# A decoder's cross attention: mask tables, normalized rows and bias additions made row by row during self attention and kept in DRAM

## The chip, the core and the metric

The kernel runs on one core of a Trainium2 chip. Its time is that of one launch on the device, in microseconds (us). The engines named below are the Tensor engine (PE, with PEld for its weight loads), the Vector engine (DVE), the Scalar engine (ACT), GpSimd (POOL) and the sync engine (SP), which issues nearly all DMA transfers. [...]

## What is computed

The reference is a decoder of two layers on x of 8 batch rows (B = 8) of 512 positions and 256 channels, all in float32. Only its first two steps matter here:

```python
x = x + _L0_attn_ref(_layernorm(x), Wq, Wk, Wv, gamma)             # self attention
x = x + _L0_xattn_ref(_layernorm(x), ctx, ctx, adj, mask, ...)     # cross attention, 16 heads of 16
```

Cross attention projects the normalized rows to queries and the context to keys and values. Its scores get the adjacency matrix added, are masked by batch row, go through a softmax over the 512 keys, weigh the values, and are projected out with a bias. After it come a local-attention transformer of two layers, an integer-quantized attention, a second cross attention and a mixture of eight experts.

## The kernel before, in words

Since exp(s + a) = exp(s) * exp(a), the kernel multiplies the exponentials of the scores by a table `share` = (mask is not 0) * exp(adj). The table depends on the batch row and is 128 partitions x 4 key tiles x 512 queries, 1 MB. The exponential of adj is taken once (`adj`, in place).

*First stage* (`stage_self_attention`, L1310). It loops over the batch rows; in iteration b it makes the scores of row b (L1395), transposes (L1362), projects (L1384) and makes the values (L1372) of row b + 1, and weighs row b (L1407). PSUM results go to SBUF alternately by ACT and DVE (`evac`, L97 to L103: sa_xnT, sa_u, sa_h). For each of four tiles, DVE takes the reciprocal of the sums and forms sa_o (L1412 to L1415), and POOL adds it to x (L1417). `means` (L1419) then takes on DVE the layer-norm statistics of the finished row for cross attention: BN statistics (L143), and a Newton iteration of tiny instructions (L1477 to L1481).

*Cross attention* (`stage_cross_attention`, L1528) is a generator. `Ahead.step(3)` in each iteration of the first stage runs it three `yield`s further, so its loads, its constants and the preparation of row 0 are spread over the first stage. After that it owns the engines. It runs 16 steps a batch row (`scores`, `soften`, `weigh`; 128 steps). A step makes four heads' scores for one key tile (PE, L1724), takes two exponentials of 128x1024 (ACT, L1735), multiplies both by `share` (DVE, L1736), and weighs the values of two steps before (PE, L1752). During the 16 steps of row b, `prepare(b + 1)` supplies small groups of calls, one group a step: loads (step 0), keys K (steps 2 and 4), the four normalizations (steps 5 and 6, L157), the bias addition `behind` (step 7, POOL, L1623), transposes T of the rows (7 and 8), queries Q (9 and 10), values V, and the four mask products M (`share`, steps 7, 9, 11, 13, DVE, L1612). These calls are `paced`: they are issued behind the multiplies of a step before.

Four steps of `weigh` give one tile of outputs and sums. The sums go through DRAM (`inverted`: sums L3302, x_sums L3303, reciprocal x_inv on DVE three steps later L3306, invs L3307) and are spread to x_wide by DMA (L1776). POOL multiplies by it (L1769). `project_out` (L1782) projects the row in steps 11 to 14 of the next row; DVE adds it to x (L1790) and takes the statistics of the next stage (L1495 to L1508). The finished x is also written to DRAM (`away`, L1797).

The buffers that matter: `x_xn` (normalized rows), `x_mask` and `x_xnT` have one or two, the tables one per parity of the batch row (`x_share0`, `x_share1`), the PSUM tag `pj` has one bank in cross attention and two in the first stage, `po` one and two. Tile pools insert the waits: a tile that takes a buffer waits for all uses of the tile before it. The order of the instructions on each engine is made by the scheduler when the program is built.

## Time and profile before

| | us |
|---|---|
| median of three runs | 3036.18 (3035.45 to 3040.28) |
| the profiled execution | 3039.56 |
| its span in the profile | 3037.8 |
| mean granted clock of PE | 0.972 of full speed |
| PE busy | 2832.6 (93%) |
| DVE busy | 2039.3 (67%) |
| ACT busy | 1191.5 (39%) |
| POOL busy | 388.1 (13%) |
| first stage ends (last weighing matmuls, L1407) | 204.2 |
| a row of cross attention (first key projection to that of the next row) | 50.7, 54.3, 54.5, 53.6, 57.9, 53.5 |

The profile is that of one execution. Its page lists busy times by engine, the span in 40 slices, the DMA queues, the chain of work that ended last, and groups of instructions by line; closer queries give the same for any window. In a timeline row, the columns are start, duration (both us), engine, line, operation, output and inputs with their shapes, and the count; the bracket gives the idle time of the engine just before and what ended it. In a row for a window, each engine has its busy time and, in brackets, its instructions, then come PE's granted clock, the mean busy share of the 16 DMA engines, and GB/s.

### The profile page before, as it was taken

The page shows a single profiled execution, that of the slowest core. Times are in us where ns is not written, and L with a number is a line of the kernel's source. Part 1 is how long each engine was busy: PE and PEld are TensorE (multiplying, and loading weights), DVE is VectorE, ACT ScalarE, POOL GpSimd, SP SyncE. Part 2 cuts the span into 40 slices and gives each one's busy share as a digit, 9 for nine tenths or more (in the row PEclk, how much of TensorE's full clock was granted, in tenths as well). Part 3 has the DMA queues.
Part 4 walks back from the last instruction along what each step waited for, and adds up shares of the span by engine and source line. Part 5 has one row for each costly group of instructions (what it writes and reads, how often), then busy time and mean ns, then how long its engine had stood idle before and what let it go on. Part 6 is the DMA issues. An engine that isn't in the chain of part 4 may idle for free. (4 is left out here: it accounts for less than half of the span.)

```text
span 3037.8 us, 39774 instructions
## 1 busy us (share of the span) xinstructions
PE 2832.6 (93%) x14929; PEld 1511.4 (50%) x14944; DVE 2039.3 (67%) x4546; ACT 1191.5 (39%) x1687; POOL 388.1 (13%) x357
## 2 busy tenths in 40 slices
PE   8999999979999999999999989998796999997998
PEld 5653333225555556555555556564444344444665
DVE  7458998977776784356776788548797766664110
ACT  2237776744444431124444431113364444441111
POOL 1111111100011110000101111101211012121111
PEclk9999999988999999999999999999897999997999
DMA  7011212101000011001000011001332132313331
GB/s 246 1 35 50 72 51 62 42 18 57 15 23 23 15 32 36 0 1 37 22 22 17 21 46 63 21 7 63 106 132 91 43 105 78 112 58 97 102 140 61
DMA packets 130694, 168.71 MB, mean 56 GB/s; under 512 B 51761, under 2 KB 79666, under 8 KB 128443
## 3 DMA queue, kind: packets, MB, share of 16 engines
q1 hardware_dynamic: 126394, 154.48, 16.3%
q0 software_dynamic: 4096, 11.59, 1.0%
q8 instruction: 119, 1.95, 0.3%
q14 instruction: 85, 0.69, 0.1%
HBM read 113.12 MB, written 47.50 MB: 53 GB/s over the span
## 5 line engine op out<-in xcount | busy, mean ns | idle before, releaser
L1889 PE MATMUL pj<-w,la_hT 128*128 128x512 f32 x720 | 334.2, 605 | 5.2 <-ACT la_qkT L1942 4.5
L1736 DVE TENSOR_TENSOR x_e<-x_e,x_share 128x1024 f32<-128x1024 f32 x256 | 315.9, 1277 | 14.3 <-ACT x_e L1735 14.1
L1735 ACT ACTIVATE x_e<-sc 128x1024 f32<-128x1024 f32 x256 | 249.2, 1023 | 83.8 <-PE sc L1724 83.8
L1889 PEld LDWEIGHTS pj<-w,la_hT 128*128 128x128 f32 x720 | 132.6, 191 | 153.4 <-issue 115.6
L2016 DVE TENSOR_TENSOR la_e<-sc,la_mask 128x1024 f32<-128x1024 f32 (+1 forms) x128 | 135.3, 1084 | 103.6 <-PE sc L2007 103.6
L3320 POOL TENSOR_TENSOR la_oT<-la_o,x_wide 128x512 f32<-128x512 f32 x64 | 97.7, 1538 | 753.1 <-DMA x_wide<-invs 678.6
L2945 ACT ACTIVATE ma_e<-sc,ma_bias 128x1024 f32<-128x1024 f32 x128 | 135.6, 1110 | 145.9 <-PE sc L2939 131.4
L2233 ACT ACTIVATE lf_gate<-pj,lf_b 128x512 f32<-128x512 f32 (+1 forms) x82 | 56.3, 687 | 333.3 <-PE pj L2212 318.0
L2020 ACT ACTIVATE la_e<-la_e 128x1024 f32<-128x1024 f32 (+1 forms) x128 | 117.5, 946 | 152.6 <-DVE la_e L2016 151.6
L2212 PE MATMUL pj<-lf_hnT,w 128*128 128x512 f32 (+1 forms) x368 | 171.4, 593 | 2.0 <-DVE lf_hid L2238 2.0
L1752 PE MATMUL po<-x_e,x_v 128*32 128x512 f32 x1024 | 140.7, 622 | 33.7 <-DVE x_e L1736 29.7
L2212 PE MATMUL sc<-lf_hnT,w 128*128 128x512 f32 x336 | 157.7, 592 | 0.0
L1724 PE MATMUL sc<-x_q,x_k 32*128 32x512 f32 x1024 | 152.9, 647 | 1.7 <-DVE sa_ok L1448 1.4
L2284 PE MATMUL po<-w,lf_hid 128*128 128x256 f32 x640 | 149.0, 379 | 0.0
L2238 DVE SCALAR_TENSOR_TENSOR lf_hid<-sc,lf_b,lf_gate 128x512 f32<-128x512 f32 x70 | 52.4, 749 | 136.4 <-PE sc L2212 133.4
L2027 PE MATMUL po<-la_e,la_v 128*64 128x256 f32 (+1 forms) x1024 | 125.8, 370 | 7.0 <-ACT la_o L2044 6.3
L2007 PE MATMUL sc<-la_qkT 64*128 64x256 f32 (+1 forms) x1024 | 128.9, 375 | 1.2 <-DVE la_e L2016 0.6
L2284 PEld LDWEIGHTS po<-w,lf_hid 128*128 128x128 f32 x640 | 117.8, 190 | 21.2 <-issue 7.4
L2939 PE MATMUL sc<-ma_qT,ma_kT 64*128 64x512 f32 x512 | 127.3, 615 | 0.4 <-ACT ma_e L2945 0.4
L2962 PE MATMUL po<-ma_e,ma_v 128*64 128x512 f32 x512 | 125.7, 612 | 0.0
L2070 PE MATMUL pj<-w,la_oT 128*128 128x256 f32 x512 | 121.0, 383 | 2.0 <-DVE lf_t L1480 0.7
L1905 DVE TENSOR_REDUCE la_ss<-la_sq 128x16 f32<-128x1024 f32 x64 | 77.7, 1215 | 65.8 <-ACT la_sq L1896 65.8
(500 smaller groups left out, 5173.6 us busy)
## 6 DMA issues: line engine op xcount, KB each, us to landing
x_wide<-invs SPq DMA_DIRECT2D x184, 128.0 KB
w<-in_f_w_dram SPq DMA_DIRECT2D x16, 1024.0 KB
kv<-kv_o SPq DMA_DIRECT2D x56, 256.0 KB
slots<-x_empty SPq DMA_DIRECT2D x8, 1028.0 KB
x_mask<-in_x_maskT_dram SPq DMA_DIRECT2D x8, 1024.0 KB
ma_kT<-kv SPq DMA_DIRECT2D x8, 1024.0 KB
ma_v<-kv SPq DMA_DIRECT2D x8, 1024.0 KB
ex_rows<-slots SPq DMA_DIRECT2D x7, 1028.0 KB
```

The source lines that it names most:

```text
L1724: nc.tensor.matmul(pair[r // 2][:, r % 2, :], d["k"][rows, g, kt * P : (kt + 1) * P], d["q"][rows, e, g, :], start=True, stop=True,)
L1735: nc.scalar.activation(ex, d["e"][rest][p], AF.Exp)
L1736: nc.vector.tensor_tensor(ex, ex, d["share"][:, kt, :].unsqueeze(1).broadcast_to([P, 2, 512]), ALU.mult)
L1752: nc.tensor.matmul(d["po"][32 * r : 32 * r + 32, :], d["v"][:, kt, 8 * g + 2 * r + e, :], ex[r // 2][:, r % 2, :], start=(kt == 0), stop=( ...
L1889: nc.tensor.matmul(ps, d["hT"][:, k, i * P : (i + 1) * P], wqkv[:, k, j * S : (j + 1) * S], start=(k == 0), stop=(k == 1),)
L2007: nc.tensor.matmul(both[half][:, r, jj * 256 : jj * 256 + to - j * P], d["qkT"][rows, 4 + c, j * P : (j + 1) * P], d["qkT"][rows, c, j * P ...
L2016: nc.vector.tensor_tensor(ex[:, :, :n_cols], ps[:, :, :n_cols], mask[:, :n_cols].unsqueeze(1).broadcast_to([P, 2, n_cols]), ALU.add,)
L2027: nc.tensor.matmul(out[:, j * P : to], lhsT(j), ex[:, jj * 256 : jj * 256 + to - j * P], start=(j == 0), stop=(j == 3), skip_group_check=True,
L2212: nc.tensor.matmul(ps[:m, :], w1[:, k, at : at + m], held[b]["hnT"][:, k, :], start=(k == 0), stop=(k == 1))
L2284: nc.tensor.matmul(ps[:, :C], held[b]["hid"][:, f, i * P : (i + 1) * P], w2[:, f, :], start=(f == 0), stop=False,)
L2939: nc.tensor.matmul(both[m // 2][:, r, :], d["k"][rows, c, kt * P : (kt + 1) * P], d["q"][rows, c, :], start=True, stop=True,)
L2945: nc.scalar.activation(ex, ps, AF.Exp, bias=bias[:, b * NST + kt : b * NST + kt + 1], scale=0.125)
```

## The change

The mask products, the normalizations and the bias additions leave `prepare`. A new function `keep(b)` makes them for one batch row as soon as `means(b)` has its statistics: it loads the mask into the tile that will hold the table, normalizes the four tiles, writes them to DRAM (`xn_kept`), adds the bias on POOL, forms the four products in place, and writes the table to DRAM (`x_tables`). `rows_done` calls it from the first stage, once the constants (`adj`, `bias`) exist. The tile is `x_tab` for odd rows; for even rows it has the tag `x_share0`, which the table of even rows in cross attention has too. The normalized rows pass through `x_xn`, one buffer, which `prepare` uses too. `prepare` now loads the table (step 2 of the row before) and the rows (step 0) instead of making them.

```diff
                 if b > 0:
                     means(b - 1)
+                    self.rows_done(b - 1)
                     ahead.step(3)
             means(B - 1)
+            self.rows_done(B - 1)
...
+    def rows_done(self, b):
+        self.due.append(b)
+        while self.due and self.keep:
+            self.keep(self.due.pop(0))
...
+        xn_kept = self.alloc(self.dram, [B, P, NST * C], F32, "xn_kept")
+        tables = self.alloc(self.dram, [B, P, NST * S], F32, "x_tables")
...
+        def keep(b):
+            share = self.alloc(first, [P, NST, S], F32, "x_tab" if b % 2 else "x_share0", bufs=1)
+            mask = share.bitcast(I32)
+            nc.sync.dma_start(mask, t["x_maskT"][b].rearrange("(k p) q -> p k q", p=P))
+            x = self.x[:, b * NST : (b + 1) * NST, :]
+            xn = self.alloc(first, [P, NST, C], F32, "x_xn", bufs=1)
+            for i in range(NST):
+                self.normalize(xn[:, i, :], x[:, i, :], self.x_ln, b * NST + i)
+            nc.sync.dma_start(xn_kept[b], flat(xn))
+            nc.gpsimd.tensor_tensor(x, x, bias.unsqueeze(1).broadcast_to([P, NST, C]), ALU.add)
+            for k in range(NST):
+                nc.vector.scalar_tensor_tensor(
+                    share[:, k, :], mask[:, k, :], 0.0, adj[:, k, :], ALU.not_equal, ALU.mult
+                )
+            nc.sync.dma_start(tables[b], flat(share))
+
+        self.keep = keep
+        while self.due:
+            keep(self.due.pop(0))
...
-                d["mask"] = self.alloc(first, [P, NST, S], I32, "x_mask", bufs=1)
-                nc.sync.dma_start(d["mask"], t["x_maskT"][b].rearrange("(k p) q -> p k q", p=P))
...
+            def share():
+                d["share"] = self.alloc(own, [P, NST, S], F32, f"x_share{b % 2}", bufs=1)
+                nc.sync.dma_start(flat(d["share"]), tables[b])
...
                 d["xn"] = self.alloc(first, [P, NST, C], F32, "x_xn", bufs=1)
+                nc.sync.dma_start(flat(d["xn"]), xn_kept[b])
...
             yield [load, rows]
             yield []
-            yield [K[0]]
+            yield [K[0], share]
             yield []
             yield [K[1]]
-            yield [normals[0], normals[1], V[0]]
-            yield [normals[2], normals[3], V[1]]
-            yield [behind, T[0], M[0]]
+            yield [V[0]]
+            yield [V[1]]
+            yield [T[0]]
             yield [T[1], V[2]]
-            yield [Q[0], M[1]]
+            yield [Q[0]]
             yield [Q[1]]
-            yield [V[3], M[2]]
-            yield []
-            yield [M[3]]
+            yield [V[3]]
```

More of the change, by code (lines that the diff above doesn't have):

```diff
@@ L1526, in clear_slots @@
         self.sent = []
+    def rows_done(self, b):
+        self.due.append(b)
+        while self.due and self.keep:
+            self.keep(self.due.pop(0))
     def stage_cross_attention(self, ahead):
         nc, t = self.nc, self.t
+        self.due, self.keep = [], None
+        xn_kept = self.alloc(self.dram, [B, P, NST * C], F32, "xn_kept")
+        tables = self.alloc(self.dram, [B, P, NST * S], F32, "x_tables")
         wq, wk, wv, wo = self.load_cross_attention()
@@ L1586, in stage_cross_attention, with flat @@
         held = {}
+        def flat(x):
+            return x.rearrange("p a n -> p (a n)")
+        def keep(b):
[16 more added lines that the diff above has]
+            keep(self.due.pop(0))
         empty = self.alloc(pool, [P, self.WIDE], F32, "x_empty", bufs=1)
@@ L1607, in load @@
                 )
-            def share(k):
-                if k == 0:
-                    d["share"] = self.alloc(own, [P, NST, S], F32, f"x_share{b % 2}", bufs=1)
-                nc.vector.scalar_tensor_tensor(
-                    d["share"][:, k, :], d["mask"][:, k, :], 0.0, adj[:, k, :], ALU.not_equal, ALU.mult
-                )
-            x = self.x[:, b * NST : (b + 1) * NST, :]
-            normals = [
-                lambda i=i: self.normalize(d["xn"][:, i, :], x[:, i, :], self.x_ln, b * NST + i)
-                for i in range(NST)
-            ]
-            def behind():
-                nc.gpsimd.tensor_tensor(x, x, bias.unsqueeze(1).broadcast_to([P, NST, C]), ALU.add)
+            def share():
+                d["share"] = self.alloc(own, [P, NST, S], F32, f"x_share{b % 2}", bufs=1)
+                nc.sync.dma_start(flat(d["share"]), tables[b])
             def rows():
                 d["xn"] = self.alloc(first, [P, NST, C], F32, "x_xn", bufs=1)
+                nc.sync.dma_start(flat(d["xn"]), xn_kept[b])
                 d["xnT"] = self.alloc(first, [P, 2, S], F32, "x_xnT", bufs=1)
@@ L1671, in prepare @@
             V = [lambda i=i: values(i) for i in range(NST)]
-            M = [lambda i=i: share(i) for i in range(NST)]
             T = [lambda c=c: turn(c) for c in range(2)]
```

## The prediction

> **What bounds the kernel now.** I read the page's chain of waits first: the Tensor engine (PE) holds 20% of it and the rest is a few per cent, so the end of each stage is set by PE and by whatever PE waits for. Only two stages are touched, so I cut the start of the span into the first stage and the rows of cross attention (a row of cross attention is 16 steps, recognised by the first key projection of L1642 at 266.4, 320.7, 375.2 us and so on).

> ```profile
> core 0: us, PE busy (x) PEld busy (x) DVE busy (x) ACT busy (x) POOL busy (x), PEclk, DMA share, GB/s
> 24.00:204.00 180.00, 179.26 (x649) 114.61 (x647) 93.58 (x380) 42.58 (x73) 24.15 (x31) 1.00 0.26 81
> ...
> 266.40:320.70 54.30, 51.23 (x315) 17.08 (x312) 48.85 (x65) 39.06 (x48) 8.00 (x3) 1.00 0.21 63
> 320.70:375.20 54.50, 51.35 (x317) 17.13 (x313) 51.10 (x73) 39.52 (x49) 7.87 (x3) 1.00 0.22 61
> 375.20:428.80 53.60, 51.26 (x317) 17.10 (x313) 50.21 (x73) 39.42 (x49) 8.38 (x3) 1.00 0.22 61
> ```

> The first stage has PE busy for 179.3 of 180 us: any stall of PE there is paid in full, though the Vector engine (DVE) is only half busy. A cross-attention row has both full: PE 51.3, DVE about 51 of 54.5. So relief of DVE is worth at most what PE idles, 54.5 - 51.3 = 3.2 us a row. PE's waits over six rows (266.4 to 594 us) say the same, all on DVE:

> ```profile
> engine line waited for: us in total, times, longest us
> PE po L1752 <- DVE x_e L1736: 9.2, 10, 2.8
> PE pj L1785 <- DVE x L1790: 4.0, 7, 0.7
> PE po L1752 <- DVE lt_ln_t L1506: 3.4, 5, 0.7
> ```

> That is 16.6 us, and row 0 (from 215.7) adds 0.3, 0.6 and 1.9.

> **What leaves cross attention.** While row b is computed, row b+1 is prepared, for b = 0 to 6 (row 0's own was prepared in the first stage already). Each time four mask products (L1612), four normalizations (L157) and one bias addition on GpSimd (POOL) go:

> ```profile
> L1612 DVE SCALAR_TENSOR_TENSOR x_share<-x_mask,x_adj 128x512 f32<-128x512 int32 x4 | 2.7, 680 | 0.0
> L157 DVE TENSOR_SCALAR x_xn<-x,x_ln_mean,x_ln_rstd 128x256 f32<-128x256 f32 x4 | 2.4, 644 | 0.0
> ```

> That is 5.1 us of DVE a row. The bias addition's price lies elsewhere:

> ```profile
> 69.96 2.40 POOL L1623 TENSOR_TENSOR x<-x,x_bias 128x1024 f32<-128x1024 f32 x1 [1.27 <-DVE x_bias L1584]
> ...
> 335.69 5.04 POOL L1623 TENSOR_TENSOR x<-x,x_bias 128x1024 f32<-128x1024 f32 x1 [3.47 <-DVE x_xn L157]
> ```

> It takes 2.4 us in the first stage and 5.0 in a busy row, and the multiplies beside it stretch: four in 6.30 us at 338.9, where pairs alone take 2.29. [...] by the row it loses 6.30 - 4.58 = 1.7. I take the row: about 6.8 us of DVE a row goes.

> But PE gets back only idle time whose cause goes. In the row from 320.7: 0.37 us at 343.0 (behind a mask product and the stretched multiplies) goes, 0.54 at 363.5 (L1790 queued behind the fourth mask product) goes; 0.45 at 359.8 stands behind a multiply stretched by another POOL operation, 1.11 at 371.4 behind L3306, which waits 0.96 us for the DMA of x_sums, 0.69 behind the Newton steps of the next stage: these stay. So 0.9, say 1.0 us a row: rows 2 to 6 give 5 us. In row 0 the 1.9 us stand behind an x_sums DMA that was late because the 1 MB mask load ran ahead of it; with that load gone I give it 1.4, and the 0.6 also goes: 2. Relief **-7 us**. Bounds: 3 (only half of this) and 16 (all idle of rows 0 and 2 to 6, 2.7 + 3.2 + 2.3 + 3.8 + 2.1 + 2.0).

> **Where the work lands.** The built program gives the order on each queue, and it differs from the words of the change. x_share0 holds row 0's reloaded table until row 0 is done, and it is also the scratch tile for rows 2, 4 and 6. So their twelve mask products are not made in the first stage but inside row 1, each four after a load of the mask into that one tile, and each load after the write of the table before. Likewise x_xn has one buffer, held by row 0 until its transposes at 139.9 us; so the normalizations of rows 1 to 4 come together at about 144 to 159 us.

> *First stage, DVE blocked on its own writes.* In row 5's scores DVE's queue now reads: normalize row 1 (4), later row 2 (4), row 3 (4), the sa_xnT eviction, row 4 (1), the sa_u eviction, row 4 (3). Each group waits for the 512 KB write of the one before. In the trace of before:

> ```profile
> 147.15 0.17 DVE L1424 COPY x_ln_rstd<-x_ln_rstd 128x4 f32<-128x4 f32 x1
> 151.32 0.69 DVE L103 COPY sa_xnT<-pj 128x512 f32<-128x512 f32 x1 [4.00 <-PE pj L1362]
> ...
> 152.12 0.19 PEld L1384 LDWEIGHTS pj<-sa_xnT,sa_wu 128*128 128x128 f32 x1 [0.24 <-DVE sa_xnT L103]
> ```

> DVE had 4.0 us free and PE took the eviction at once (no slack). A 512 KB write: the "away" write was issued at 313.25 and its bytes were through by 315.5; a small write takes 1.7 us from issue (sums, 269.07) to the next queue entry that needs it (270.77), so 1.7 + 1.4 = 3.1 us. Row 1's group (4 x 0.36 = 1.5 us) ends DVE's work at 148.7, row 2's at 150.2, row 3's can start at 150.2 + 3.3 = 153.5 and ends at 155.0: sa_xnT 3.6 us late. **+3.6** (bounds 1 and 7, by one write more or less). sa_u's wait then falls inside PE's own shift.

> *First stage, the mask products of rows 1, 3, 5, 7* (2.7 us each). Put on DVE's timeline of before: row 1's, at 38.7, push an eviction of po, 0.3 us; row 3's wait for a mask that SP issues only after the table of row 1 is written (42.0 + 4.6 + 5.5 = about 53), about 1.0 us before sa_u; row 5's fall into 70.4 to 75, where 1.07 us are free before sa_xnT: 1.0 with the gaps of the Newton chain; row 7's stand between two releases of po (two banks) at 86 to 90: 1.6. **+3.9** (bounds 1 and 8). The bias additions, 2.4 us each, fit into POOL's gaps of 6 to 18 us between the x additions. SP's new waits hold up only slot clearing and next weights there; neither is due.

> *Boundary.* Row 7's four normalizations stand between the last statistics (211.2 us) and the first multiply (211.31), for which PE was waiting (3.69 us idle at 213.8): 4 x 0.36 = **+1.5**.

> *Row 1.* One chain decides, since the tile is one: load the mask, four products (2.7 us), write the table, load the next mask, and so on. A 1 MB mask load that was issued at 254.50 shows its length:

> ```profile
> 254.00:255.00 1.00, 0.90 (x8) 0.16 (x8) 1.00 (x2) 1.00 (x3) 0.00 (x0) 1.00 0.00 0
> ...
> 257.00:258.00 1.00, 1.00 (x12) 0.21 (x8) 1.00 (x2) 1.00 (x2) 0.00 (x0) 1.00 1.00 367
> ...
> 260.00:261.00 1.00, 1.00 (x12) 0.31 (x8) 1.00 (x2) 0.94 (x2) 0.00 (x0) 1.00 0.01 2
> ```

> The bytes are through by 259.6, so I count 5.5 us to use; a write is 1.7 + 2.9 = 4.6 (1 MB at 367 GB/s). From row 0's last multiply (261.3): mask 267.0, products 269.7, written 274.4, mask 279.9, products 282.6, written 287.2, mask 292.7, products 295.4, and then the multiply of step 22, ready at 297.7. DVE stands still meanwhile, and behind it wait the multiplies that PE's weighing needs: step 17's by 271.6 (ready 272.0), step 20's by 281.9 (ready 284.9), step 22's by 288.3 (it waited until 289.3). So PE ends 9.4 us late there, **+8.4** beyond its old idle; later steps only lose slack that PE-bound rows have. [...] my five transfers are 25.7 us[...] With 1.2 us more a transfer it is +14. [...]

> *Reloads.* Each row now loads its table (1 MB) and its rows (512 KB) from DRAM. A table is issued at step 2 of the row before and first used 14 steps (some 46 us) later, the rows after the last transposes and used most of a row later: 5.5 and 3.1 us, hidden, zero. They stand in SP's queue among the x_wide and x_sums transfers, whose reciprocal comes three steps (10 us) later; the mask load that goes had the same size there. If that cover fails, 1 us a row, 6 in all; the same at the gain side, if the mask loads were what made x_sums late. After cross attention PE's and ScalarE's order is unchanged.

> **Sum.** -7 + 3.6 + 3.9 + 1.5 + 8.4 = +10.4 us on the profiled execution's 3039.6 (span 3037.8 and 1.8 around it): 3050.0. That execution lies 3.4 above the median 3036.2, so the median becomes 3046.6.

> **Rivals.** 0.2% (6 us) is about what a measurement of this kernel can tell from no change.

> *Forecast, chance 0.5:* about 3046.6; by its bounds 3040 to 3053.

> *Slower still, 0.15.* The transfers are longer than one alone shows, because they meet slot clearing (DMA at 1.0 busy until 60 us in the page's slices) in the first stage and x_oT and x_wide in row 1, and every leg is paid by a standing DVE. For it: the chain is serial and SP issues in order. Against: row 1's DMA share is only 0.21. Row 1 +14, the first stage's stalls 12 in place of 7.5, boundary 1.5, relief -5: +22, 3058.

> *Faster, 0.2.* DVE's relief in rows 0 and 2 to 6 gives back all of PE's idle time, because what I call unrelated waits are DVE's accumulated lateness. For it: DVE is at 94% in the row from 320.7, and every PE wait names it. Against: DVE itself idles in each row (1.2 us for x_sums, 1.2 for ScalarE), so its lateness is drained. Price: -16, with the added stalls at their lower side (first stage 3.5, boundary 1.5, row 1 +3): -8, 3028. The point from which it decides: with the added 17.4 us as computed, 2.9 us a row must come back in six rows, nearly all that is idle; with stalls at 8, 1.4 us are enough.

> *A draw, 0.15.* Relief and stalls cancel, for instance since DVE's waits in row 1 take the place of waits that it had there (2.83 us for x_sums at 272.6): within 4 us, 3036.

> That the change does not do what it says holds in part by the order of the queues (rows 2, 4, 6) and is in the forecast.

> **Numbers.** Slower: 0.45 of the forecast's 0.5 and the 0.15, 0.6; same: 0.05 and the 0.15, 0.2; faster 0.2. The range leaves out half of the faster case and a quarter of the slower one: 3027 to 3061.

> **What would show it.** Around 150 us: sa_xnT about 3.6 us late behind an x_xn normalization that waits for xn_kept. From 266: three groups of mask products in row 1, each behind a wait for a mask load, and that row some 8 us longer than 54.3. Rows 2 to 6 at about 53, DVE there near 46 busy and multiplies nearer 1.14 than 1.29 us. First multiply at about 220 instead of 211.3. I am wrong if the groups in row 1 find their masks there, if rows 2 to 6 shrink to 51.5, or if the half-speed clock (0.94 in the row from 428.8) falls elsewhere, which is worth 3 us either way.

## The result, and the profile after

The kernel after takes 3043.11 us in the median of ten launches (3041.16 to 3049.64), the kernel before, launched beside it, 3036.61 (3030.28 to 3041.62). The ratio is 1.0025, with a 95% interval of 1.0015 to 1.0036: the change makes this kernel about 7 us slower.

The first view is again the table by stage, with the rows of cross attention cut at their first key projections (now L1663, at 225.2, 275.2, 342.3, 394.6, 446.8, 499.4 and 551.6 us).

```profile
core 0: us, PE busy (x) PEld busy (x) DVE busy (x) ACT busy (x) POOL busy (x), PEclk, DMA share, GB/s
24.00:204.00 180.00, 174.76 (x620) 109.89 (x619) 109.29 (x406) 42.30 (x73) 34.99 (x34) 0.99 0.46 153
225.24:275.17 49.93, 49.35 (x300) 15.44 (x297) 36.40 (x34) 38.34 (x48) 6.91 (x3) 0.96 0.19 58
275.17:342.28 67.11, 56.05 (x317) 17.81 (x313) 51.38 (x70) 39.64 (x49) 2.56 (x2) 0.90 0.46 156
342.28:394.59 52.31, 51.26 (x317) 17.10 (x313) 45.38 (x65) 39.28 (x49) 3.31 (x2) 1.00 0.25 72
394.59:446.77 52.18, 51.32 (x316) 17.16 (x312) 45.31 (x65) 39.07 (x49) 3.08 (x2) 1.00 0.24 72
```

Row 1 went from 54.3 to 67.1 us, and not by idle time alone: with the same work (317 matmul records, 315 before; a few can be missing from a trace) PE is busy for 56.0 us instead of 51.2, and its mean clock there is 0.90. Rows 2 and 3 went from 54.5 and 53.6 to 52.3 and 52.2, with DVE at 45.3 to 45.4 instead of 50 to 51. The first stage has PE busy for 4.5 us less in the same 180.

PE's waits from 270 to 610 us show where the relief is:

```profile
PE po L1770 <- DVE x_e L1754: 12.1, 7, 6.3
PE po L1770 <- DVE lt_ln_t L1508: 3.9, 6, 0.7
PE po L1770 <- ACT x_o L1776: 0.3, 1, 0.3
```

Of the 12.1 us, 10.3 are three waits in row 1. The waits for the additions to x (4.0 us before) are gone, and what rows 2 to 6 keep is nearly all the Newton steps of the next stage, which the prediction had named as staying. DVE's timeline of row 1 shows the chain through one tile:

```profile
276.81 2.50 DVE L1613 SCALAR_TENSOR_TENSOR x_share<-x_share,x_adj 128x512 f32<-128x512 int32 x4 [2.89 <-DMA x_share<-in_x_maskT_dram]
...
289.16 2.50 DVE L1613 SCALAR_TENSOR_TENSOR x_share<-x_share,x_adj 128x512 f32<-128x512 int32 x4 [3.05 <-issue]
...
301.44 2.50 DVE L1613 SCALAR_TENSOR_TENSOR x_share<-x_share,x_adj 128x512 f32<-128x512 int32 x4 [5.14 <-DMA x_wide<-invs]
```

Three groups of four products, 12.3 us apart, each behind a wait of DVE. Only the first bracket names the mask load. The other two name "issue" and x_wide, but what the three waits share is a mask load still under way. In DVE's queue the multiplies behind them waited too: ACT had written the exponentials for the multiply at 303.86 by 299.28, and DVE did nothing from 296.30 to 301.44. SP issued the mask loads at 271.57, 283.57 and 295.56, the second only after the table's write:

```profile
271.57 0.39 SPq L1605 DMA_DIRECT2D x_share<-in_x_maskT_dram  x1
...
279.33 0.34 SPq L1616 DMA_DIRECT2D x_tables<-x_share  x1
...
283.57 0.40 SPq L1605 DMA_DIRECT2D x_share<-in_x_maskT_dram  x1
```

So a load took 5.2 to 5.9 us until the products ran, and the next load went 4.2 us after the write was issued. PE waited 3.40 us until 281.63 and 6.34 us until 306.27.

The stall in the first stage, on DVE and then on PE:

```profile
151.51 1.37 DVE L157 TENSOR_SCALAR x_xn<-x,x_ln_mean,x_ln_rstd 128x256 f32<-128x256 f32 x4
...
155.61 1.38 DVE L157 TENSOR_SCALAR x_xn<-x,x_ln_mean,x_ln_rstd 128x256 f32<-128x256 f32 x4 [2.65 <-DMA xn_kept<-x_xn]
156.91 0.69 DVE L103 COPY sa_xnT<-pj 128x512 f32<-128x512 f32 x1
...
157.65 4.45 PE L1384 MATMUL pj<-sa_xnT,sa_wu 128*128 128x512 f32 x6 [3.78 <-DVE sa_xnT L103]
```

The eviction of sa_xnT comes at 156.91 in place of 151.32, and PE waited 3.78 us for it.

### The profile page after: what moved, and what is told of

The parts are those of the page before. It is cut to its first block, busy times and chain, and to the rows that moved or that the text cites. A ratio compares the mean times of both kernels' runs of the same rounds, so it can differ in the third digit from the quotient of the medians.

```text
span 3040.1 us, 39875 instructions
## 1 busy us (share of the span) xinstructions
PE 2827.6 (93%) x14944; PEld 1506.2 (50%) x14944; DVE 2030.9 (67%) x4546; ACT 1190.3 (39%) x1687; POOL 379.2 (12%) x357
## 5 line engine op out<-in xcount | busy, mean ns | idle before, releaser
L1907 PE MATMUL pj<-w,la_hT 128*128 128x512 f32 x720 | 333.9, 604 | 5.2 <-ACT la_qkT L1960 4.5
L1754 DVE TENSOR_TENSOR x_e<-x_e,x_share 128x1024 f32<-128x1024 f32 x256 | 309.5, 1256 | 32.3 <-ACT x_e L1753 32.1
L1907 PEld LDWEIGHTS pj<-w,la_hT 128*128 128x128 f32 x720 | 132.4, 191 | 153.2 <-issue 114.1
L2256 DVE SCALAR_TENSOR_TENSOR lf_hid<-sc,lf_b,lf_gate 128x512 f32<-128x512 f32 x70 | 52.3, 747 | 135.2 <-PE sc L2230 135.2
```

The lines of the kernel that those rows point to most:

```text
L1754: nc.vector.tensor_tensor(ex, ex, d["share"][:, kt, :].unsqueeze(1).broadcast_to([P, 2, 512]), ALU.mult)
L1907: nc.tensor.matmul(ps, d["hT"][:, k, i * P : (i + 1) * P], wqkv[:, k, j * S : (j + 1) * S], start=(k == 0), stop=(k == 1),)
```

## The clock that a wait leaves behind

The extra 4.8 us of PE time in row 1 have one place. Windows cut around the two long waits:

```profile
281.00:288.00 7.00, 6.37 (x26) 1.36 (x27) 5.11 (x5) 1.94 (x2) 0.00 (x0) 0.56 0.77 260
288.00:304.00 16.00, 11.36 (x72) 3.77 (x70) 9.69 (x14) 10.08 (x13) 0.00 (x0) 1.00 0.43 148
304.00:312.00 8.00, 5.73 (x24) 2.12 (x24) 6.85 (x7) 1.26 (x2) 0.00 (x0) 0.57 0.72 259
```

PE came back at 281.63 and at 306.27, and each time it first ran at about half speed: the eight weighing matmuls behind the second wait take 1.94 us, those of a step before it 1.06. The clock record of after has a spell (a stretch that it gives as half speed) that begins within each of the four long waits up to here: from 157.50 for 3.41 us, from 218.94 for 10.24, from 280.38 and 304.28 for 6.83 each, where the waits end at 157.65, 223.38, 281.63 and 306.27. The lengths are 3.41 us or a multiple of it. In the traces of before and after, from 24 us on, all 22 waits of PE of 3.0 us or more overlap a spell or have one within 1.2 us behind them, and so do 17 of the 22 waits between 2.0 and 3.0 us. The kernel before has such a case: the 57.9 us of its row from 428.8 hold a wait of 2.84 us until 480.9 and a spell of 6.83 us from 479.77. In row 1 of after PE worked for 5.6 and 4.8 us inside its two spells (clock 0.50), and its busy time grew by 4.8: a long wait cost itself plus about half of that part of the spell in which PE worked, which the prediction's sums left out.

The clock also hides a part of the loss in this pair of profiles. By the start of the next stage (its first use of la_hT) the kernel after is 10.0 us behind (616.1 against 606.1), at the end of the span only 2.3 us (3040.1 against 3037.8). In between lies this, first before, then after, at the same point of the work:

```profile
677.00:702.00 25.00, 20.68 (x55) 12.60 (x54) 12.68 (x52) 0.58 (x1) 2.76 (x6) 0.52 0.17 55
```
```profile
687.00:712.00 25.00, 18.89 (x72) 10.69 (x72) 15.54 (x58) 4.63 (x9) 2.76 (x6) 1.00 0.38 127
```

In the profiled execution of before PE had half its clock for 23.9 us there, with waits of only 0.5 to 0.7 us between groups of four matmuls (2.07 us a group, 1.13 in the kernel after). From the first of these groups to the same later matmul (L1889, now L1907) it took 24.9 us (678.0 to 702.9), the kernel after 16.6 (687.4 to 704.0). So 8.3 us of the 10.0 are made up there. The change touches nothing at that place, and the profiled execution of the run with the later reload (below) has a spell of about that length there too (its groups take 1.82 to 2.08 us from 671 on). The medians are the better measure of the whole, the traces of the parts.

## The experiments

All times are ratios to the kernel before, launched on the same chip; a tenth of a per cent is 3 us. The table gives the places in the profiles at which the runs differ (us): the first key projection of row 1's pass, the length of row 1, of rows 2 to 5 together, and the first use of la_hT.

| run | to row 1 | row 1 | rows 2-5 | la_hT | ratio (95% interval) |
|---|---|---|---|---|---|
| before | 266.4 | 54.3 | 219.5 | 606.1 | 1 |
| after | 275.2 | 67.1 | 209.3 | 616.1 | 1.0025 (1.0015 to 1.0036) |
| one scratch tile | 275.6 | 54.6 | 209.3 | 604.1 | 0.9990 (0.9980 to 0.9999) |
| own rows | 270.1 | 66.9 | 209.6 | 611.8 | 1.0013 (1.0002 to 1.0024) |
| both | 272.4 | 55.7 | 209.9 | 602.7 | 0.9973 (0.9962 to 0.9985) |
| both, last row late | 272.3 | 56.1 | 209.5 | 602.3 | 0.9979 (0.9969 to 0.9989) |
| both, reload later | 271.8 | 52.5 | 210.1 | 600.2 | 0.9954 (0.9937 to 0.9971) |
| the same, bias in the row | 273.0 | 52.9 | 209.5 | 599.4 | 0.9975 (0.9966 to 0.9984) |
| the same, placed by hand | 279.3 | 53.1 | 209.2 | 607.4 | 1.0004 (0.9996 to 1.0012) |
| tables only | 271.3 | 57.4 | 210.8 | 603.3 | 0.9985 (0.9975 to 0.9994) |
| rows and bias only | 269.2 | 52.8 | 213.4 | 601.3 | 0.9960 (0.9945 to 0.9976) |
| the same, products earlier | 270.6 | 53.0 | 211.6 | 600.6 | 0.9967 (0.9953 to 0.9980) |

**One scratch tile.**

```diff
-            share = self.alloc(first, [P, NST, S], F32, "x_tab" if b % 2 else "x_share0", bufs=1)
+            share = self.alloc(first, [P, NST, S], F32, "x_tab", bufs=1)
```

> The kernel after, with one tile (x_tab) as scratch for the tables of all rows, so that no table's scratch waits for row 0's own table; every table is made in the first stage. Theory (row 1 of cross attention is held by the chain mask load, products, table write in one tile): row 1 falls from 67.1 us to about 53, since its 10.3 us of PE waits shrink to about 1 and the two half-speed spells behind them (6.8 us each, 3.4 us lost each) go as well; the twelve products of rows 2, 4 and 6 cost up to 3 us in the first stage. Against the kernel after: -8 to -14 us; against the kernel before: -2 to -8. Rival (row 1's waits come from something else, late x_sums transfers or the reloads in SP's queue): row 1 keeps more than 5 us of PE waits and the time changes by less than 3 us.

The window of row 1 in this run, with the columns of the tables above:

```profile
275.62:330.18 54.56, 51.40 (x317) 17.17 (x313) 43.29 (x57) 39.77 (x49) 3.65 (x2) 1.00 0.24 70
```

Row 1 fell by 12.5 us to 54.6, its clock is back at 1.00, and of its waits 2.9 us are left (one of 2.28, not the 1 us foreseen). The whole kernel fell by about 10.6 us against after (1.0025 - 0.9990). The chain through the tile was row 1's loss, and one name for the tile takes it away. The twelve products more in the first stage cost little: row 1 starts 0.4 us later than in after.

**Own rows.**

```diff
-            xn = self.alloc(first, [P, NST, C], F32, "x_xn", bufs=1)
+            xn = self.alloc(first, [P, NST, C], F32, "x_xk", bufs=1)
...
-                d["ctxT"] = self.alloc(first, [P, 2, S], F32, "x_ctxT")
+                d["ctxT"] = self.alloc(first, [P, 2, S], F32, "x_ctxT", bufs=1)
```

> The kernel after, with a buffer of its own (x_xk) for the normalized rows that are written away, and one buffer in place of two for x_ctxT to make room. Theory (DVE stands at about 150 us because the normalizations of rows 1 to 4 share x_xn with row 0 and wait for each other's writes): the 3.8 us wait of PE near 157.7 us goes, and the half-speed spell at 168 with it: -4 to -6 us against the kernel after. Rival (the four normalizations in DVE's queue ahead of the eviction are the delay themselves): an eviction is late by 1.5 us in each row, and the time changes by less than 2 us.

The 3.78 us wait went and row 1 starts 5.0 us earlier. The ratio fell by 0.0012, 3.6 us, but its interval and that of after overlap: the gain is shown by the trace, not by the times alone. A new wait of 1.43 us appears near 79 us, where row 1's normalizations now stand ahead of sa_xnT. The theory holds; the rival takes back a part.

**Both.** The two edits together.

> Both edits: one scratch tile for all tables, and an own buffer for the rows that are written away. Theory (the two stalls are independent, each is paid in full): about -14 to -18 us against the kernel after, so -8 to -12 against the kernel before: about 3027. Rival (the relief in the later rows was lateness that the stall in row 1 had merely moved): rows 2 to 6 grow back from 52.3 towards 54 us, and the time stays within 4 us of the kernel before.

0.0052 under after, 16 us, and 8 us under before. Rows 2 to 6 do not grow back: the relief is real, and the two stalls add up (10.6 and 3.6 us alone, 16 together, within what the intervals leave open).

**Both, last row late.**

```diff
             means(B - 1)
-            self.rows_done(B - 1)
...
+                if i == 6:
+                    paced(lambda: self.keep(B - 1))
                 if i == 1:
                     ahead.step()
```

> As the run with both edits, but the last row's share (mask load, normalizations, bias addition, products) is issued in step 6 of cross attention's row 0, not at the end of the first stage. Theory (the last row's normalizations stand ahead of the first multiply, and its bias addition runs beside the first multiplies): the first multiply comes 1.4 us earlier against the end of the first stage, PE waits 3.7 us there and not 5.1, and the half-speed spell behind it is shorter (3.4 us, not 10.2): -1 to -5 us against the run with both edits. Rival (row 0 then loses the same on DVE): DVE's 4 us come into row 0 and PE waits there; 0 +- 1.5 us.

PE waits 3.70 us at the first multiply, as before the change, in place of 5.11. But row 0 has a new wait of 1.28 us, and the time is the same: the rival. What is taken from the boundary comes back in the row (50.4 us from its first key projection to the next, 49.4 in the run with both edits).

**Both, reload later.**

```diff
-                nc.sync.dma_start(flat(d["share"]), tables[b])
+                with self.tc.issue_after(self.newest(mybir.EngineType.SP)):
+                    nc.sync.dma_start(flat(d["share"]), tables[b])
...
-            yield [K[0], share]
-            yield []
+            yield [K[0]]
+            yield [share]
```

It rests on SP's queue in the run with both edits, at the start of row 1:

```profile
268.74 0.33 SPq L1643 DMA_DIRECT2D x_share<-x_tables  x1
269.16 0.38 SPq L3325 DMA_DIRECT2D invs<-x_inv  x1
273.73 1.71 SPq L1794 DMA_DIRECT2D x_wide<-invs  x4
```

The small invs transfer goes behind the 1 MB table, and x_wide, which needs it, can go only 4.6 us later; the x_sums after it is late too, and DVE stands for 5.71 us.

> As the run with both edits, but the table's reload is issued a step later and behind the newest transfer in SP's queue, so in row 1 it comes behind the reciprocals' transfers (invs, x_wide) and not ahead of them. Theory (in row 1 the 1 MB reload ahead of invs makes x_sums 3 us late, and DVE stands 5.8 us and PE 2.2 us): DVE's wait near 280 us falls to about 3 us, PE's wait of 2.2 us near 284 goes and the half-speed spell at 294 with it: -2 to -4 us against the run with both edits. Rival (x_sums is late there for another reason, the reloads are hidden): PE's wait stays over 1.5 us and the time is within 1.5 us.

```profile
268.40 0.33 SPq L3326 DMA_DIRECT2D invs<-x_inv  x1
269.83 1.71 SPq L1795 DMA_DIRECT2D x_wide<-invs  x4
271.59 0.43 SPq L1644 DMA_DIRECT2D x_share<-x_tables  x1
```

Now x_wide follows invs after 1.4 us, DVE waits 4.03 us instead of 5.71, x_sums goes at 277.51 and not at 279.65, PE's wait of 2.2 us has shrunk to 0.5, and row 1 has 52.5 us instead of 55.7. The ratio is lower too, by 0.0019, but with six launches its interval overlaps that of the run with both edits. In rows 2 to 6 the reload stood behind invs already. So one reload was not hidden: the prediction's zero was wrong there by about 3 us, which in the kernel after lay beneath the mask chain.

**Tables only, rows and bias only.** One part of the change each: in the first, keep makes only the table (one scratch tile) and prepare has normals and behind as before; in the second, keep makes only the rows (x_xk) and the bias, and prepare has x_mask and the four products M in steps 7, 9, 11 and 13.

> Only the tables of the change, with one scratch tile for all rows: the mask products are made in the first stage, while normalizations and bias additions stay in the row before. Theory (relief goes by DVE's time, of which the products are 2.7 us of 6.8 a row): PE waits in rows 2 to 6 about 1.8 us a row, between the 2.8 of before and the 0.9 of after; no added wait at the first multiply (3.7 us as before); the first stage keeps the delays of the products. About 3036: +2 to +5 us against the run with both edits, -1 to -6 against the kernel before. Rival (the products alone make the multiplies late): rows 2 to 6 as in the kernel after (52.2 to 52.7 us), and the time is at or under the run with both edits.

> Only the rows and the bias of the change, with own buffers: normalizations and bias additions are made in the first stage, the mask products stay in the row before (x_mask is loaded there, no tables are kept). Theory (relief goes by DVE's time): PE waits in rows 2 to 6 about 1.6 us a row; the first stage loses less than 3 us (no products there); the first multiply is 1.4 us later; row 1 has no reload of a table: -2 to -6 us against the kernel before, +2 to +5 against the run with both edits. Rival (the products alone make the multiplies late): rows 2 to 6 as before (53.5 to 54.5 us), and the time is at or over the kernel before.

DVE's busy time in a row is nearly the same in both (48.7 and 47.6 us in their row 2), but PE's waits in rows 2 to 6 are not: 5.4 us with the products gone and 9.5 us with the rows and the bias gone, of 13.4 before. So relief does not go by DVE's time. In the whole the second part has the lower ratio, though the two intervals just touch. What speaks for it in the traces: it has no table traffic, no wait in row 1 as long as that of the other (2.42 us), and only 2.6 us more of waits up to row 0 than the kernel before.

**Products earlier.**

```diff
-            yield [V[0]]
-            yield [V[1]]
-            yield [T[0], M[0]]
-            yield [T[1], V[2]]
-            yield [Q[0], M[1]]
+            yield [V[0], M[0]]
+            yield [V[1], M[1]]
+            yield [T[0]]
+            yield [T[1], V[2], M[2]]
+            yield [Q[0], M[3]]
             yield [Q[1]]
-            yield [V[3], M[2]]
-            yield []
-            yield [M[3]]
+            yield [V[3]]
```

> As the run with only the rows and the bias moved, but the four mask products stand in steps 5, 6, 8 and 9 of the row before, not in steps 7, 9, 11 and 13, where they share DVE's queue with project_out's additions to x. DVE's work is the same. Theory (what PE waits for in a row is decided by which DVE instruction stands ahead of the one that frees pj or feeds a weighing, not by DVE's busy time): the 4.0 us of PE waits for the additions (7 waits in rows 1 to 6) fall below 1.5 us, rows 2 to 6 go from 53.0 to 53.6 us to about 52.6; -2 to -4 us against the run with only the rows moved, about 0.995 of the kernel before. Rival (DVE's busy time decides, 47.7 us a row): the waits turn up at other places and the time is within 1.5 us of that run.

PE's waits on the additions and the multiplies in rows 1 to 6, before this edit and with it:

```profile
PE pj L1803 <- DVE x L1808: 4.0, 7, 0.8
PE po L1770 <- DVE x_e L1754: 3.0, 5, 0.9
```
```profile
PE pj L1801 <- DVE x L1806: 4.1, 6, 1.0
PE po L1768 <- DVE x_e L1752: 0.4, 1, 0.4
```

My theory fell: the waits for the additions stay, though no product stands near them. What stands there is

```profile
408.62 0.25 DVE L3322 RECIPROCAL x_inv<-x_sums 128x16 f32<-128x16 f32 x1 [3.01 <-DMA x_sums<-sums]
```

with the multiplies queued behind it, and then the addition. With the products out of its way DVE only reaches that reciprocal earlier and waits there: its waits for x_sums in rows 1 to 6 grew from 12.5 to 27.3 us. Of the waits for multiplies 2.6 us went, and the ratio is the same within the intervals.

**Bias in the row.** As the run with the later reload, with the bias addition back in step 7.

> As the run with the later reload, but the bias addition stays in step 7 of the row before. Theory (it costs DVE 1.7 us a row beside it, and PE a wait only where a multiply is late): multiplies beside it stretch to about 1.5 us, rows 2 to 6 get 0.3 to 0.6 us of PE waits more each, row 7's addition no longer runs beside the first multiplies: 0 to +3 us. Rival 1 (with DVE at 45 of 52 us all of it is hidden): within 1 us. Rival 2 (the addition is what made the multiplies late in the kernel before): rows 2 to 6 over 53 us, +5 us or more.

Rows 2 to 5 are 0.6 us shorter, not longer, and la_hT starts 0.8 us earlier: the first rival, all of it is hidden. The ratios differ by 0.002 nonetheless, and their intervals meet. Nothing in the rows accounts for that, and behind la_hT it is the profiled execution with the later reload that loses some 7 us, by a spell of half speed of about 24 us (from 671 on). The difference stays open.

**Placed by hand.** As the run with the later reload; keep for rows 1 to 5 is called between the values and the weighing, behind the newest DVE instruction, and for rows 6 and 7 in steps 5 and 9 of row 0.

```diff
+                if b > 2:
+                    with self.tc.issue_after(self.newest(mybir.EngineType.DVE)):
+                        self.rows_done(b - 2)
                 weigh(b)
...
+                if i in (5, 9):
+                    paced(lambda: self.keep(B - 2 + (i == 9)))
```

> As the run with the later reload, but the shares of rows 1 to 5 are issued behind the evictions of the next row's values, and those of rows 6 and 7 in steps 5 and 9 of cross attention's row 0. Theory (normalizations and products ahead of sa_xnT, and the last row's ahead of the first multiply, are what the first stage pays): the waits of 1.45 and 1.47 us near 54 and 80 us go, PE waits 3.7 us and not 5.1 at the first multiply: -3 to -6 us against the run with the later reload, about 0.994 of the kernel before. Rival (the same DVE work then stands ahead of the reciprocals that free po, or ahead of row 0's multiplies): new waits of PE of 1 to 3 us there, and the time is within 2 us.

The rival again: eight operations in one block stand ahead of sa_o, and PE waits six times for it, 8.2 us in all, where the run with both edits has two such waits of 1.2 us in sum: there the scheduler had slipped the products in between. At the first multiply PE waits 4.1 us instead of 5.1, but row 0 has new waits. Two kinds of PE's waits up to 280 us:

```profile
PE po L1407 <- DVE sa_o L1415: 8.2, 6, 1.9
PE po L1774 <- DVE x_e L1758: 7.5, 4, 4.1
```

**A long wait on purpose.** Two kernels add idle work on DVE to step 8 of rows 2 to 6 of the run with both edits: three maxima of x_adj with itself (DVE is busy for 51.7 us a row in rows 2 to 5, 45.3 in rows 2 and 3 of after), and one reduction over x_adj read four times (8.68 us).

> The run with both edits, plus three maxima of x_adj with itself (128x2048, about 2.28 us each) on DVE in step 8 of each of rows 2 to 6; they change nothing in the result. Theory (a wait of PE of about 3 us or more is followed by a spell of half speed some 6 to 13 us later, which costs 1.7 to 5 us more than the wait): each of the five blocks makes PE wait 3 to 5 us at one place, and a spell of 3.4 to 10.2 us follows within 15 us of each; rows of about 59 us, and +25 to +40 us in all. Rival (spells come by themselves, by the load or by chance): rows 2 to 6 have none or one spell, as in the run with both edits, and the five blocks cost their waits alone, +15 to +20 us.

> As the run with three maxima in step 8 of rows 2 to 6, but in their place one reduction on DVE over x_adj read four times (128x8192, about 9 us in one instruction), so that PE must wait at one place. Theory (a wait of PE of about 3 us or more is followed by a spell of half speed): PE waits 4 to 7 us once in each of the five rows, and within 15 us of each a spell of 3.4 to 10.2 us follows, 5 of 5; rows of about 60 us; +30 to +45 us against the run with both edits. Rival (the spells come by themselves): at most one spell in rows 2 to 6, each row longer by its wait alone (56 to 58 us), +20 to +30 us.

The maxima were no block: the scheduler put two multiplies between the second and the third. PE waited 2.1 us at the most, no spell came (clock 1.00 in rows 2 to 5, and the eight matmuls behind that wait took 1.06 us), and some 32 us of DVE work (five times 6.4) cost 0.0041, 12.5 us (ratio 1.0014, 1.0005 to 1.0023). The precondition of my theory was not met, so this run does not speak on it, except that about three fifths of the work fit into DVE's slack. The long reduction settles it (ratio 1.0123, 1.0109 to 1.0138). Windows around the first of its five waits, which ended at 359.42:

```profile
354.00:359.00 5.00, 0.27 (x4) 0.00 (x0) 5.00 (x3) 2.52 (x4) 0.00 (x0) 1.00 0.09 21
359.00:364.00 5.00, 4.58 (x16) 1.44 (x20) 4.97 (x6) 0.09 (x1) 0.00 (x0) 0.66 0.00 0
364.00:369.00 5.00, 5.00 (x32) 1.93 (x28) 2.36 (x2) 4.33 (x6) 0.05 (x1) 1.00 0.31 60
```

and two lines of PE's timeline there:

```profile
359.42 1.93 PE L1770 MATMUL po<-x_e,x_v 128*32 128x512 f32 x8 [5.14 <-DVE x_e L1754]
...
364.87 1.06 PE L1770 MATMUL po<-x_e,x_v 128*32 128x512 f32 x8
```

## Why the prediction was right, point by point

The sign and the mechanism hold: work moved early did not all arrive early, because it queued for two buffers, and the stalls cost more than the relief gave back. The size holds too: +10.4 was the sum, +10.0 stands at the end of cross attention in the traces, +6.5 in the medians. By place, the traces give +9.6 up to row 0 (predicted +9.0), -0.8 in row 0 (-2), +12.8 in row 1 (+8.4) and -11.6 behind it (-5). The two large errors, in row 1 and in the rows behind it, have opposite signs and nearly cancel: that the sum came so close is luck.

| step | predicted | measured |
|---|---|---|
| DVE blocked on its own writes | +3.6 | PE wait 3.78, and a 3.4 us spell behind it; -5.0 to row 1 without it |
| products of rows 1, 3, 5, 7 | +3.9 | two waits of PE, 0.35 and 0.38 |
| (not in the sum) row 6's bias addition at 205 us | 0 | waits of 0.93 and 0.27 |
| boundary | +1.5 | wait 5.11 for 3.69: +1.4; first multiply at 220.9, foreseen at 220 |
| row 1's chain | +8.4 | waits 10.98 for 3.07: +7.9; PE busy +4.8 |
| relief, row 0 | -2 | waits 0.58 for 2.73: -2.2; but PE busy +1.7, as the spell behind the boundary reaches into it |
| relief, rows 2 to 6 | -5 | waits 3.9 for 13.4: -9.5, and a spell gone: PE busy -2.7 |
| reloads | 0 | 0 in after, about 3 in row 1 once the chain is gone |

*The chain in row 1* was right in place, count and length: three loads, the second and the third each behind the write of the table before. The transfers were estimated at 5.5 us (measured 5.2 to 5.9) and 4.6 us (3.9 to 4.2); the five together took 24.8 us, where the prediction had 25.7. The lower sides that it gave the chain (+3 in the faster case) were estimates of mine that no trace shows. What was mis-sized is its price, because half-speed spells followed two of the waits. *The relief* was mis-sized the other way. I had let 0.45 us (behind a stretched multiply) and 1.11 us (behind a reciprocal that waits for x_sums) stay, as having causes of their own; both went. The rival that all idle time comes back was nearer to the rows than my term: rows 2 to 6 came to 52.2 to 52.6 us, close to the 51.5 that I had named as the mark against me. It failed as a whole because the stalls were not at their lower side: row 1 grew by 12.8 us, where that rival had +3. *The products in the first stage* were overrated five times: the scheduler splits the four and puts them between the tiny steps of the Newton iterations. *The bias addition* was overlooked at one place: beside row 6's at 205.10, a 128x1 product on DVE took 1.76 us instead of 0.16, and sa_o came late. *The stall at 150 us* was right in cause and size, though its working sets 3.3 us for a write that it had found to take 3.1; measured from one write's issue (152.92) to the next group (155.61) it was 2.7. (The remark that the DMA engines are full until 60 us holds in windows of 10 us, 0.8 to 1.1 of their time; the page's first slice, 76 us wide, has 0.7.)

What is not settled: how the 6.5 us of the medians relate to the 10.0 of the traces at la_hT. The profiled pair shows one reason, 8 us lost to the clock in the next stage in one execution, but how often each kernel has that spell was not counted.

## What to carry to other kernels

Work that left a full engine gave back only the waits behind it (9.5 us of PE's in rows 2 to 6), and work that is moved early is early only if its buffers are free: here the tag of one scratch tile sent three of the eight tables back into the stage that was to be relieved, and one name for all of them turned +7 us into a small gain. Look at the order on each queue and at who holds each buffer before counting instructions. Price a wait of PE of several us at itself plus the slower work after it (here 5.7 and 1.6 us); and when a large transfer is put into a queue, see which small, urgent one comes behind it.

The runs point to two versions that beat both kernels: the whole change with one scratch tile, own rows and the later reload, and the move of the rows and the bias alone. Their intervals overlap; the second has less traffic.

## What the runs showed of the hardware

- The times of launches of one and the same kernel go with the clock that PE was granted: over 58 launches of the kernel before (3030.5 to 3048.2 us) the correlation of time with the clock lost (the share not granted, times the span: 64 to 85 us) is 0.88, at 0.58 us for each us of clock lost. A difference of 3 us is small against this spread and needs many launches.
- Half speed was also seen without a long wait: in the stretch of before at 677 us above, it lasted for 23.9 us (from 677.75) although PE never waited more than 0.7 us from 664 to 702, while the same work in after ran at full speed (clock 1.00, 1.13 us a group of four in place of 2.07).
- Two bias additions of after ran beside work on DVE:

```profile
205.10 2.35 POOL L1611 TENSOR_TENSOR x<-x,x_bias 128x1024 f32<-128x1024 f32 x1 [5.06 <-DVE x_xn L157]
...
221.10 8.87 POOL L1611 TENSOR_TENSOR x<-x,x_bias 128x1024 f32<-128x1024 f32 x1 [3.84 <-DVE x_xn L157]
```

  Beside the first, which took 2.35 us, stood small DVE instructions, and a 128x1 product at 205.70 took 1.76 us instead of 0.16. The second began 0.2 us after a run of six multiplies on DVE (220.88 to 227.77, 1.15 us each, not stretched), ended 2.2 us after the last of them, and took 8.87 us, nearly four times as long. More than these two cases is not shown.
